# A single-core recurrent block: a written-out order of 2633 pieces of work, searched anew with other hand-over times

## The chip, the cores and the metric

The kernel runs on one NeuronCore of a Trainium2 chip. That core has a matrix engine (TensorE, PE in the profile, with its weight loads shown apart as PEld), a vector engine (DVE), an activation engine (ACT), a general-purpose engine (POOL) and a sync engine (SP) that here only issues transfers. Each engine works through its own instructions in the order in which they were emitted, and waits in front of an instruction until what it needs from other engines is there. The metric is the device time of one execution in microseconds; lower is better.

## The reference, cut to what matters

The block is one RWKV-like layer on 8 sequences of 256 tokens with 512 channels (32 heads of 16), all in fp32:

```python
xn = ln(x, ln1_w, ln1_b);  sx = token_shift(xn, state[:, 1])
xxx = tanh((xn + sx * maa_x) @ maa_w1).reshape(b, l, 5, 1, 32)
x5  = xn[:, :, None] + sx[:, :, None] * (maa_stack + (xxx @ maa_w2))
w = exp(-exp(time_decay + tanh(x5[:, :, 1] @ decay_w1) @ decay_w2))
r, k, v = x5[:, :, 3] @ Wr.T, x5[:, :, 0] @ Wk.T, x5[:, :, 2] @ Wv.T
g = silu(x5[:, :, 4] @ Wg.T)
def step(s, (r_t, k_t, v_t, w_t)):            # 256 steps, state 16 x 16 for each head
    a = k_t[..., :, None] * v_t[..., None, :]
    return a + w_t[..., None] * s, einsum("bhk,bhkd->bhd", r_t, u * a + s)
att = group_norm(outs) * gn_w + gn_b
x = x + (att * g) @ Wo.T
xn2 = ln(x, ln2_w, ln2_b);  sx2 = token_shift(xn2, state[:, 0])
rr = sigmoid((xn2 + sx2 * ffn_maa_r) @ Wfr.T)
kk = square(relu((xn2 + sx2 * ffn_maa_k) @ Wfk.T))
return x + rr * (kk @ Wfv.T)
```

## The kernel before, in words

**Three stages for each sequence.** The work of a sequence (a "batch" in the names, 0 to 7) is cut into three stages. `inputs_of_scan` makes the layer norm, the token shift, the five mixed inputs and the projections k, v, r, g and w. `scan` runs the recurrence in four blocks of 128 rows; each block has four groups, and for a group a broadcast load brings v from DRAM into a buffer `vs`, DVE multiplies it by k (L849), DVE scans over time (L851), POOL multiplies the scanned states by r (L854), and PE sums over the state with a selection matrix (the "gather", L862). `rest` makes the group norm, the product with Wo, the second layer norm and the feed-forward part. Stages of up to three sequences lie side by side in time.

**Pieces.** Nothing is issued where it is written. Each call (`plan.add`) notes a piece: an engine, an assumed duration, the buffers it writes and reads, and a function that issues it. There are 2633 pieces. Buffers come from small pools: six PSUM buffers `ps` for nearly all matmul results, one larger PSUM buffer `wrep` for the decay factors of the scan, six `vs` buffers, six `st8` buffers for scanned states (called `st` in the profile), fourteen `mix` buffers and some others. A piece that needs a buffer waits until its last user is done.

**What sets the order.** `order` is a list scheduler. It takes the ready piece with the lowest rank from a heap, gives it the earliest start that its engine, its inputs and its buffers allow, and picks the buffers. The ranks are a table of numbers, `TURNS`, one row for each stage. The earliest start is worked out with a few assumed times: `LATENCY` (from the end of a piece on one engine until another engine may start on its result), `AHEAD` (added where PE is the receiver), `GAP` (between two dependent pieces on one engine) and `SWITCH` (a change of the activation table on ACT, and of the tile shape on PE). In the end all pieces are sorted by the planned start and emitted so. Therefore the table and the assumed times set three things only: the order of the pieces on each engine, which buffer each piece gets, and, in `tiles`, whether a matmul with full-width weights is issued as one wide or four narrow instructions. On the chip an instruction starts when what it waits for is there, whatever the plan assumed.

**Names that follow.** The matmuls are issued by a helper, so most stand at one line (L398) and are told apart by tiles: `mix,mw` is the first mixing product of a batch (its result goes to `ta` by a tanh on ACT, L651), `ta,mw2a` the second, whose results ACT and DVE turn into the mixed inputs (L674, L676). `tb,mw2b` is the product for the fifth mixed input. `mix` with `Wk`, `Wv`, `Wr`, `Wg` are the projections, which ACT copies out of PSUM (L757, L787). `Ws` are streamed weights: with `g` it is the product with Wo, with `mix` the feed-forward products; ACT evacuates them with a relu (L943) or a sigmoid into `o` (L952). L912 to L928 belong to the group norm: ACT copies rows of the reciprocal (`sq`, `rk`, L917), POOL multiplies (L919, L928). ACT also makes `wrep` (L832), the first column of each `vs` (L842), and copies to `att` (L812). SP issues all loads and stores but `vo`, which ACT issues.

Of the kernel before, what the change touches and what calls it, by code (L numbers as in the profile page):

```python
# [67 lines left out]
class Plan:  # L68
# [4 lines left out]
    LATENCY = {"PE": 0.12, "DVE": 0.09, "ACT": 0.09, "POOL": 0.09, "DMA": 1.65}  # L73
    LANDS = {"vs__": (2.3, 1.8), "rsb_": (0.2, 1.9), "sq_": (0.2, 1.9), "s": (0.2, 1.9), "vo_": (0.75, 2.2), "vo__": (0.38, 2.2), "o_": (0.75, 1.1), "x": (1.6, 1.7), "xt": (1.6, 1.7)}
    SWITCH = {"ACT": 1.3, "PE": 0.12}
    AHEAD = {"PE": 0.2}
    GAP = {"PE": 0.0, "DVE": 0.16, "ACT": 0.04, "POOL": 0.11, "DMA": 0.03}
# [37 lines left out]
    def stage(self):  # L115
# [964 lines left out]
```

## Time and profile before

| | |
|---|---|
| median of 3 runs | 617.36 us (617.15 to 620.06) |
| profiled execution, its own time | 618.31 us |
| span of its trace | 616.4 us |
| granted TensorE clock | 1.00 |
| PE busy | 594.5 us, 96% |
| DVE busy | 542.2 us, 88% |
| POOL busy | 518.0 us, 84% |
| ACT busy | 511.6 us, 83% |
| PE busy between 50 and 550 us | 491.01 of 500 us |
| PE busy from 564 us on | 47.76 of 52.4 us |

Busy time is the sum of the time in which an engine executes; an engine waits in the rest. Where two numbers stand behind a row of the timeline they are the start and the length in microseconds; a bracket at the end of a row gives the idle time just before it and the engine and line that ended it. Rows of like instructions in a line are put together, with their number behind an x.

### The profile page before, as it was taken

Reading aid. Unit: us, or ns where it says so; the run is one execution under the profiler, and the core shown is the slowest. Engines: PE = TensorE matmul, PEld = TensorE weight load, DVE = VectorE, ACT = ScalarE, POOL = GpSimd, SP = SyncE. Lnnn points to the kernel's source line nnn. Section 1 sums busy time; section 2 is a strip of 40 time slices with the busy share of each in tenths; the row PEclk is TensorE's granted clock in tenths of the full one; section 3 lists DMA queues with packets and bytes.
Section 4 is the critical chain, followed back from the end, with each engine's and each line's share of the span. In section 5 each row is a group of like instructions: output and inputs, shape, how many; then the busy total and the mean of one; then the engine's idle time right before and its main releaser. Section 6 shows DMA issues by size and latency. Waiting matters only on the chain.

```text
span 616.4 us, 18782 instructions
## 1 busy us (share of the span) xinstructions
PE 594.5 (96%) x7856; PEld 341.6 (55%) x7856; DVE 542.2 (88%) x490; ACT 511.6 (83%) x1164; POOL 518.0 (84%) x414
## 2 busy tenths in 40 slices
PE   5999999899999999999999999999999999999997
PEld 5675556456544674367543664465754464446464
DVE  5689999999999998799989999999999999895441
ACT  3888679989999989989999888999889789965431
POOL 1799999999999988899889999999889998887030
PEclk9999999999999999999999999999999999999999
DMA  8897779687778787758787697677876698861542
GB/s 287 265 242 171 214 192 231 163 233 181 185 202 235 206 206 214 197 154 221 202 240 206 197 248 202 184 230 218 224 194 193 185 252 245 225 193 66 165 145 85
DMA packets 52499, 124.83 MB, mean 203 GB/s; under 512 B 5824, under 2 KB 11200, under 8 KB 52416
## 3 DMA queue, kind: packets, MB, share of 16 engines
q1 hardware_dynamic: 48048, 119.46, 71.4%
q10 hardware_dynamic: 4368, 4.20, 2.1%
q8 instruction: 61, 1.00, 0.7%
q14 instruction: 22, 0.18, 0.1%
HBM read 115.25 MB, written 8.39 MB: 201 GB/s over the span
## 4 chain that ended last, share of the span: by engine, by line
PE 61%; ACT 17%; DVE 7%; POOL 7%; DMA 5%; issue 3%; SPq 0%; ACTq 0%; DVEq 0%; POOLq 0%
PE ps L398 51%; PE ps L862 5%; DMA vs<-vo 4%; POOL st L854 4%; DVE st L851 3%; ACT sq L917 2%; ACT rk L917 2%; PE ps L574 2%; PE ps L726 2%; DVE vs L849 2%; ACT att L812 1%; ACT wrep L832 1%; ACT ps L674 1%; ACT mix L605 1%; ACT vs L842 1%
## 5 line engine op out<-in xcount | busy, mean ns | idle before, releaser
L851 DVE TENSOR_TENSOR_SCAN st<-wrep,vs 128x1024 f32<-128x1024 f32 x128 | 289.2, 2277 | 4.9 <-ACT wrep L832 1.9
L854 POOL TENSOR_TENSOR st<-st,r 128x1024 f32<-128x1024 f32 x128 | 254.3, 2003 | 11.0 <-DVE st L851 9.5
L849 DVE TENSOR_TENSOR vs<-vs,ps 128x1024 f32<-128x1024 f32 x122 | 143.7, 1205 | 9.7 <-ACT vs L842 8.5
L398 PE MATMUL ps<-Ws,mix 128*32 128x512 f32 (+2 forms) x864 | 114.9, 589 | 1.9 <-ACT o L952 1.0
L398 PEld LDWEIGHTS ps<-Ws,mix 128*32 128x32 f32 (+1 forms) x864 | 37.8, 116 | 65.3 <-issue 58.2
L686 POOL TENSOR_TENSOR mix<-mix,xn 128x512 f32<-128x512 f32 x62 | 66.6, 1095 | 2.8 <-DVE mix L680 2.0
L588 POOL TENSOR_TENSOR sx<-xn 128x512 f32<-128x512 f32 x30 | 31.5, 1061 | 38.0 <-ACT xn L584 37.9
L862 PE MATMUL ps<-st,con 128*32 128x256 f32 x1024 | 62.1, 381 | 1.2 <-POOL st L854 1.0
L398 PE MATMUL ps<-mix,Wv 128*32 128x256 f32 (+1 forms) x688 | 59.8, 380 | 0.0
L398 PE MATMUL ps<-mix,Wr 128*32 128x256 f32 (+1 forms) x760 | 59.3, 380 | 0.0
L398 PE MATMUL ps<-mix,Ws 128*32 128x256 f32 (+1 forms) x736 | 57.8, 380 | 1.3 <-issue 0.7
L398 PE MATMUL ps<-mix,Wk 128*32 128x256 f32 (+1 forms) x952 | 59.0, 379 | 0.0
L398 PE MATMUL ps<-mix,Wg 128*32 128x256 f32 (+1 forms) x712 | 58.7, 379 | 0.0
L398 PE MATMUL ps<-Ws,g 128*32 128x512 f32 (+1 forms) x464 | 56.7, 593 | 1.5 <-POOL g L928 1.5
L607 POOL TENSOR_TENSOR mix<-mix,xn 128x512 f32<-128x512 f32 x44 | 47.5, 1092 | 6.1 <-ACT mix L605 6.1
L398 PEld LDWEIGHTS ps<-mix,Ws 128*32 128x32 f32 (+1 forms) x736 | 42.0, 120 | 15.7 <-ACT o L952 1.5
L674 ACT ACTIVATE ps<-ps,vec 128x256 f32<-128x256 f32 x112 | 46.6, 444 | 4.6 <-PE ps L398 3.2
L398 PEld LDWEIGHTS ps<-mix,Wv 128*32 128x32 f32 (+1 forms) x688 | 40.6, 123 | 15.2 <-issue 1.0
L812 ACT COPY att<-ps 32x256 f32<-32x256 f32 x128 | 46.4, 363 | 2.8 <-POOL g L928 0.7
L862 PEld LDWEIGHTS ps<-st,con 128*32 128x32 f32 x1024 | 32.3, 110 | 29.5 <-issue 6.5
L398 PEld LDWEIGHTS ps<-mix,Wr 128*32 128x32 f32 (+1 forms) x760 | 38.7, 119 | 17.8 <-issue 0.8
L398 PEld LDWEIGHTS ps<-mix,Wg 128*32 128x32 f32 (+1 forms) x712 | 39.1, 122 | 16.7 <-ACT xn L584 0.6
(123 smaller groups left out, 952.5 us busy)
## 6 DMA issues: line engine op xcount, KB each, us to landing
vs<-vo SPq DMA_DIRECT2D x128, 512.0 KB, 5.8
Ws<-in_fr SPq DMA_DIRECT2D x16, 512.0 KB, 6.5
Ws<-in_wo SPq DMA_DIRECT2D x16, 512.0 KB, 5.6
Ws<-in_fk SPq DMA_DIRECT2D x16, 512.0 KB, 5.8
Ws<-in_fv SPq DMA_DIRECT2D x16, 512.0 KB, 5.4
x<-in_x SPq DMA_DIRECT2D x9, 512.0 KB, 6.3
vo<-v ACTq DMA_DIRECT2D x15, 256.0 KB, 4.9
out<-o SPq DMA_DIRECT2D x15, 256.0 KB, 4.7
```

What stands on the lines that cost most here:

```text
L398: nc.tensor.matmul(out[i : i + n], lhsT=w[:, i : i + n], rhs=x, start=first, stop=final)
L574: nc.tensor.transpose(ps()[:, m, n * P : (n + 1) * P], xh[n]()[:, k * P : (k + 1) * P], idt())
L588: take(512, [sx], [xn], lambda xn=xn, sx=sx, e=nc.vector if alone and q else nc.gpsimd: e.tensor_tensor(sx(), xn()[:, :, 0:T], xn()[:, :, ...
L607: gp(512, t, [t, xn[q]], lambda q=q, t=t: nc.gpsimd.tensor_tensor(t(), t(), xn[q]()[:, :, 1 : T + 1], ALU.add))
L674: act(256, p_, [p_, vec], lambda g=g, q=q, m=m, p_=p_: nc.scalar.activation(p_()[:, m, :], p_()[:, m, :], AF.Identity, bias=col(f"maa_{g}" ...
L686: gp(512, t, [t, xn[q]], lambda q=q, t=t: nc.gpsimd.tensor_tensor(t(), t(), xn[q]()[:, :, 1 : T + 1], ALU.add))
L812: act(350, atts[q], [pc], lambda i=32 * (2 * q + m), m=m, q=q, h=32 * h: nc.scalar.copy(atts[q]()[h : h + 32, m, :], pc()[i : i + 32, 0, :]))
L849: dve(4 * T, [vs], [vs, kp], lambda m=m, vs=vs, kp=kp: nc.vector.tensor_tensor(vs(), vs(), kp()[:, m : m + 1, :].to_broadcast([P, 4, T]), ...
L851: dve(4 * T, [st], [w, vs], lambda w=w, vs=vs, st=st: nc.vector.tensor_tensor_scan(st().rearrange("p n t -> p (n t)"), w().rearrange("p n ...
L854: gp(4 * T, st, [st, r], lambda m=m, st=st, r=r: nc.gpsimd.tensor_tensor(st(), st(), r()[:, m : m + 1, :].to_broadcast([P, 4, T]), ALU.mul ...
L862: nc.tensor.matmul(pat()[32 * i : 32 * i + 32, 0, :], lhsT=con()[:, s : s + 32], rhs=done[i]()[:, j, :], start=(j == 0), stop=(j == 3),)
L917: act(256, rsb, [rs], lambda blk=2 * q + n, n=n, rows=rows, rsb=rsb: nc.scalar.copy(by_block(rsb)[rows, n, :], rs()[32 * blk : 32 * blk + ...
```

## The change

Only assumed times and the ranks change. The pieces, their assumed durations, the pools and the code that issues them are the same; the table `TURNS` is replaced as a whole (its first two lines are shown).

```diff
-    LATENCY = {"PE": 0.12, "DVE": 0.09, "ACT": 0.09, "POOL": 0.09, "DMA": 1.65}
+    LATENCY = {"PE": 0.25, "DVE": 0.13, "ACT": 0.14, "POOL": 0.06, "DMA": 1.65}
-    SWITCH = {"ACT": 1.3, "PE": 0.12}
-    AHEAD = {"PE": 0.2}
-    GAP = {"PE": 0.0, "DVE": 0.16, "ACT": 0.04, "POOL": 0.11, "DMA": 0.03}
+    SWITCH = {"ACT": 1.38, "PE": 0.11}
+    AHEAD = {"PE": 0.1}
+    GAP = {"PE": 0.0, "DVE": 0.16, "ACT": 0.08, "POOL": 0.12, "DMA": 0.03}
...
     TURNS = """
-        7 135 8 30 33 47 70 145 79 48 121 116 189 225 137 147 149 159 4 5 16 6 34 35 36 37 43 31 38 56 32 46 60,
-        0 1 2 9 3 10 11 12 13 14 20 21 22 23 27 15 17 18 19 24 28 29 25 26 39 40 45 63 87 94 96 95 97 107 64 66 73 74
...
+        13 19 16 27 30 99 87 111 97 83 112 28 228 50 21 56 142 156 2 3 17 9 39 46 38 41 47 36 40 49 37 58 59,
+        0 1 4 5 6 7 8 10 11 12 23 31 32 34 35 14 18 22 24 25 42 43 29 33 44 45 48 65 103 104 108 105 107 116 66 78 80
...
```

What the two orders look like beside each other is shown at three places, which the prediction comes back to. In these rows the numbers behind a name tell buffers apart.

**Place 1: POOL ahead of the last gather of batch 0.** The names: `st` times `r` (L854) are the products behind the scan, `mix` plus `xn` (L686) are the mixed inputs of batch 2, `rk` (L799) and `att` (L818) belong to the scan of batch 1. Before:

```order
L686 TENSOR_TENSOR mix_109<-mix_109,xn_99 128x512
L818 TENSOR_TENSOR att_139<-v_129,att_139 128x2x256
L854 TENSOR_TENSOR st_156<-st_156,r_126 128x1024
L799 TENSOR_TENSOR rk_150<-r_125,k_124 128x512
L686 TENSOR_TENSOR mix_116<-mix_116,xn_99 128x512
L686 TENSOR_TENSOR mix_106<-mix_106,xn_99 128x512
L854 TENSOR_TENSOR st_157<-st_157,r_126 128x1024
L854 TENSOR_TENSOR st_152<-st_152,r_126 128x1024
L854 TENSOR_TENSOR st_153<-st_153,r_126 128x1024
```

and after:

```order
L686 TENSOR_TENSOR mix_109<-mix_109,xn_99 128x512
L686 TENSOR_TENSOR mix_113<-mix_113,xn_99 128x512
L854 TENSOR_TENSOR st_156<-st_156,r_126 128x1024
L686 TENSOR_TENSOR mix_116<-mix_116,xn_99 128x512
L854 TENSOR_TENSOR st_157<-st_157,r_126 128x1024
L854 TENSOR_TENSOR st_152<-st_152,r_126 128x1024
L854 TENSOR_TENSOR st_153<-st_153,r_126 128x1024
L686 TENSOR_TENSOR mix_117<-mix_117,xn_99 128x512
L799 TENSOR_TENSOR rk_150<-r_127,k_123 128x512
```

The product `rk` moved from ahead of the last three `st` products of that gather to behind them; one 128x512 piece less stands in front of them.

**Place 2: PE around the first mixing product of batch 4** (`mix,mw`). `Ws,mix` with 32x512 are the halves of the two sigmoid products of batch 1; `ta,mw2a` is the second mixing product of batch 4. Before:

```order
L398 MATMUL ps_174<-mix_111,Ws_165 32x256 x8
L398 MATMUL ps_174<-mix_118,Ws_166 32x256 x8
L398 MATMUL ps_169<-mix_107,mw_66 32x256 x8
L398 MATMUL ps_169<-mix_115,mw_66 32x256 x8
L398 MATMUL ps_170<-Ws_164,mix_110 32x512 x8
L398 MATMUL ps_170<-Ws_167,mix_106 32x512 x8
L398 MATMUL ps_174<-Ws_164,mix_110 32x512 x8
L398 MATMUL ps_174<-Ws_167,mix_106 32x512 x8
L398 MATMUL ps_173<-ta_120,mw2a 64x256 x2
L398 MATMUL ps_170<-ta_120,mw2a 64x256 x2
```

and after:

```order
L398 MATMUL ps_174<-Ws_164,mix_119 32x512 x8
L398 MATMUL ps_170<-Ws_164,mix_119 32x512 x8
L398 MATMUL ps_172<-mix_115,mw_66 32x256 x8
L398 MATMUL ps_172<-mix_113,mw_66 32x256 x8
L398 MATMUL ps_170<-Ws_165,mix_111 32x512 x8
L398 MATMUL ps_174<-Ws_165,mix_111 32x512 x8
L398 MATMUL ps_170<-ta_120,mw2a 64x256 x2
```

Two of the four halves moved ahead of the mixing product. In both orders the second mixing product writes to `ps_170` early, which the first sigmoid product had filled.

**Place 3: ACT around the two sigmoids of batch 2** (`o`), with the tanh of batch 5 (`ta`) near them. Before:

```order
L917 COPY sq_159<-sq_158 32x256 x6
L605 ACTIVATE mix_106<-sx_102,vec 128x256
L812 COPY att_138<-ps_169 32x256
L842 ACTIVATE vs_147<-s_82,cm_83 128x4
L787 ACTIVATE g_135<-ps_171 128x512
L952 ACT_TABLE_LOAD
L952 ACTIVATE o_162<-ps_173 128x512
L952 ACTIVATE o_163<-ps_170 128x512
L651 ACTIVATE ta_120<-ps_171 128x256
L832 ACT_TABLE_LOAD
L832 ACTIVATE wrep_168<-w_133 128x4x255
```

and after:

```order
L812 COPY att_138<-ps_169 32x256
L842 ACTIVATE vs_147<-s_81,cm_83 128x4
L812 COPY att_138<-ps_169 32x256
L917 COPY sq_159<-sq_158 32x256
L917 COPY rk_150<-sq_158 32x256
L952 ACT_TABLE_LOAD
L952 ACTIVATE o_162<-ps_172 128x512
L952 ACTIVATE o_163<-ps_170 128x512
L842 ACTIVATE vs_148<-s_81,cm_83 128x4
L832 ACT_TABLE_LOAD
L832 ACTIVATE wrep_168<-w_133 128x4x255
L812 COPY att_138<-ps_169 32x256
```

Three of the `att` copies that stood behind the sigmoids stand ahead of them now (a fourth was ahead already), and the tanh, which is the next row after those shown, comes behind `wrep`. The first mixing product of batch 5 (`ps_171` before) has `ps_170` now, the buffer that the second sigmoid frees.

234 rows, old and new, of the table TURNS are left out of this document.

## The prediction

> **What bounds the kernel now.** I read the busy line of the page first, then the busy time by stretches of the span, then PE's waits, and the timeline around each of them.
>
> ```profile
> PE 594.5 (96%) x7856; PEld 341.6 (55%) x7856; DVE 542.2 (88%) x490; ACT 511.6 (83%) x1164; POOL 518.0 (84%) x414
> ```
>
> ```profile
> 7.29:50.00 42.71, 41.76 (x512) 31.08 (x520) 33.14 (x55) 32.38 (x79) 30.74 (x29) 1.00 0.94 267
> 50.00:550.00 500.00, 491.01 (x7055) 273.12 (x7039) 477.50 (x392) 450.84 (x1035) 465.24 (x358) 1.00 0.78 208
> 550.00:564.00 14.00, 14.00 (x86) 11.69 (x79) 12.24 (x9) 8.56 (x19) 13.57 (x11) 1.00 0.19 57
> 564.00:616.40 52.40, 47.76 (x232) 25.70 (x224) 17.09 (x30) 18.25 (x31) 7.98 (x8) 1.00 0.40 135
> ```
>
> The columns are the stretch, its length, the busy time of PE, PEld, DVE, ACT and POOL, then clock, DMA share and GB/s. PE is the bound, and nearly nothing is left: it idles 500.00 − 491.01 = 9.0 us between 50 and 550, about 1 us of the 42.71 before, nothing in the 14 us before the last gather, and 4.6 us after 564, where the same pieces follow in almost the same order in both versions. DVE idles 22.5 us in the middle. A gain must therefore come out of PE's 9.0 us, and its waits show whom PE waits for:
>
> ```profile
> PE ps L398 <- ACT r L757: 1.9, 1, 1.9
> PE ps L398 <- issue: 1.6, 2, 0.9
> PE ps L398 <- POOL g L928: 1.5, 2, 0.9
> PE ps L398 <- ACT o L952: 1.2, 2, 1.0
> PE ps L862 <- POOL st L854: 1.0, 1, 1.0
> PE ps L574 <- ACT xh L558: 0.6, 1, 0.6
> PE ps L398 <- POOL mix L607: 0.5, 1, 0.5
> PE ps L398 <- ACT mix L943: 0.3, 1, 0.3
> ```
>
> (total, times, longest; 50 to 550 us). These are 8.6 of the 9.0 us, in eleven waits of 0.2 to 1.9 us. ACT and POOL are themselves nearly full there, 90% and 93%, so a wait ends when an in-order queue has worked off what stands ahead of one piece. That is what a new order changes.
>
> **What moves.** The work is the same. The tile form changes for a few full-width pieces (four narrow instructions or one wide for the same columns), and PE changes its tile shape 107 times instead of 105. A gather takes 1.73 us, and 1.86 behind a change:
>
> ```profile
> 56.23 1.73 PE ps L862 x32
> 501.33 1.86 PE ps L862 x32
> ```
>
> so the two changes cost 2 x 0.13, about **+0.2** (estimate). The number of table loads on ACT stays the same. Otherwise pieces change places by a few rows; the summed work ahead of each of the 32 gathers differs by under 4 us on PE and on DVE, mostly by nothing. So I go from wait to wait, count by durations of the trace what more or less stands ahead, and carry the waits on.
>
> *The gather at 96.75 (place 1).*
>
> ```profile
> 90.76 5.93 POOL L854 TENSOR_TENSOR st<-st,r 128x1024 f32<-128x1024 f32 x3
> 96.75 1.71 PE L862 MATMUL ps<-st,con 128*32 128x256 f32 x27 [1.04 <-POOL st L854]
> 88.38 4.46 DVE L851 TENSOR_TENSOR_SCAN st<-wrep,vs 128x1024 f32<-128x1024 f32 x2
> L686 POOL TENSOR_TENSOR mix<-mix,xn 128x512 f32<-128x512 f32 x62 | 66.6, 1095 | 2.8 <-DVE mix L680 2.0
> ```
>
> PE waits 1.04 us for the last of three products of POOL, which follow one another without a gap. One piece of 128x512 less (1.1 us by the group of L686, on average) stands ahead, so they end about 1.05 earlier; the last scan ends at 92.84 and leaves room for it (with one product of 5.93 / 3 = 2.0 us behind it, 94.8). **−1.0**; bounds −1.0 and 0, if POOL meets a late input there.
>
> *From 236 to 247 (place 2).*
>
> ```profile
> 236.09 1.93 PE L398 MATMUL ps<-mix,mw 128*32 128x256 f32 x32 [0.54 <-POOL mix L607]
> 237.84 7.05 PE L398 MATMUL ps<-Ws,mix 128*32 128x512 f32 x64
> 244.30 0.60 ACT L952 ACTIVATE o<-ps 128x512 f32<-128x512 f32 x1
> 245.01 1.12 PE L398 MATMUL ps<-ta,mw2a 32*64 32x256 f32 x32
> 247.16 1.06 PE L398 MATMUL ps<-Ws,mix 128*32 128x512 f32 x8 [1.03 <-ACT o L952]
> ```
>
> Two of the four sigmoid halves (7.05 / 4 = 1.76 each) move ahead of the mixing product, 3.5 us of work, while its input from POOL gets about 2.0 later (one more 2.0 us product ahead): the wait of 0.54 goes. But the next waits are set by ACT. Its first `o` gets about 0.5 later (`ta` moves back by about 0.85, one row copy of 0.40 goes from between). It ended at 244.90 and frees `ps_170`, so the second mixing product starts at about 245.5, though PE would be there at 244.5; the second `o`, on which 247.16 hangs, moves by the same 0.5. The 0.54 saved is waited off here, and 0.5 more: **+0.5**. Bounds: −0.5, if ACT is not late, and +0.9.
>
> *From 312 to 317 (place 3).*
>
> ```profile
> 309.92 1.28 ACT L952 ACT_TABLE_LOAD   x1
> 311.21 1.09 ACT L952 ACTIVATE o<-ps 128x512 f32<-128x512 f32 x2
> 312.35 3.66 PE L398 MATMUL ps<-mix,Ws 128*32 128x256 f32 x64 [0.17 <-ACT o L952]
> 312.65 1.28 ACT L832 ACT_TABLE_LOAD   x1
> 314.05 1.03 ACT L832 ACTIVATE wrep<-w 128x1020 f32<-128x1020 f32 x1
> 317.38 1.93 PE L398 MATMUL ps<-mix,Ws 128*32 128x256 f32 x32 [0.32 <-ACT mix L943]
> ```
>
> The pair of sigmoids gets three `att` copies (0.36 each by their record), two row copies and one small piece more ahead and three small pieces fewer, together about +1.1 us. The mixing product of batch 5 now goes into the buffer that the second sigmoid frees, at about 312.3 + 1.1 = 313.4, while PE comes there at about 312.2: a wait of 1.2 in place of 0.17. The tanh behind it goes back by 1.28 + 1.03 = 2.3 us and a copy, and its taker on PE comes behind products of 3.66 us, which cover that. I take **+0.5**, half, because I cannot see whether ACT, which has small waits of its own ahead, carries the whole 1.1 on; bounds −0.5 (both waits gone) and +1.6.
>
> *The other waits of PE.*
>
> ```profile
> 541.15 2.35 PE L398 MATMUL ps<-Ws,mix 128*32 128x512 f32 x20 [0.85 <-issue]
> 480.07 2.35 PE L398 MATMUL ps<-Ws,g 128*32 128x512 f32 x20 [0.93 <-POOL g L928]
> 136.17 1.09 PE L574 MATMUL ps<-idt,xh 128*128 128x128 f32 x8 [0.57 <-ACT xh L558]
> 115.42 0.69 PE L398 MATMUL ps<-tb,mw2b 32*64 32x256 f32 x16 [1.88 <-ACT r L757]
> ```
>
> The first row's releaser is not seen; the sigmoid that comes before it on ACT gets 3.4 us less ahead: **−0.85**, bounds −0.85 and 0. The other wait without a releaser (1.6 − 0.9 = 0.7, at 453) stands before a product whose two halves change places: **0**, bounds −0.7 and +0.7. At 480 the chain runs over ACT (affine, then POOL's product), with about 0.7 more ahead on ACT: **+0.3**, bounds 0 and +0.7. At 136 ACT has 0.3 to 0.5 more ahead: **+0.2**, bounds 0 and +0.5. At 115 PE makes r before k and v now, but on ACT both copies stand together behind the same `wrep`: **0**, bounds −1.9 (the wait goes) and +0.4.
>
> *Loads.*
>
> ```profile
> 92.86 9.60 DMA vs<-vo
> ACT vs L842 <- DMA vs<-vo: 2.0, 4, 0.9
> ```
>
> The load that the chain of waits shows with 9.60 us landed behind a load of x for the next product with Wo; in the new order that load of x goes out much earlier, into the head, and another one later. ACT waited 2.0 us in all, in four pieces of 0.5 on average; one of them moves: **−0.5**, bounds −2.0 and +0.6 (another load in the way, one more such piece). In the head the earlier order of the constants keeps its loads in time by my count, 0.
>
> **The sum**: +0.2 − 1.0 + 0.5 + 0.5 − 0.85 + 0 + 0.3 + 0.2 + 0 − 0.5 = −0.65 us. The profiled execution took 618.31 us, of which 616.4 are the span and 1.9 lie around it; it becomes 617.7. It lies 0.95 above the median of 617.36, and against that the sum gives **616.7 us**. About 0.5% (3.1 us) is what a measurement can tell from no change, so this is "the same". With all lower bounds the sum is −7.25, with all upper ones +5.6.
>
> **The rivals.**
>
> *R1, faster: the new times are truer, and the search finds what I cannot follow by hand.* For it speaks a hand-over in the head:
>
> ```profile
> 13.81 1.89 PE L398 MATMUL ps<-mix,mw 128*128 128x256 f32 x8
> 15.74 0.38 ACT L651 ACTIVATE ta<-ps 128x256 f32<-128x256 f32 x1 [0.29 <-PE ps L398]
> 16.17 0.67 PEld L398 LDWEIGHTS ps<-ta,mw2a 32*64 32x64 f32 x32 [0.22 <-ACT ta L651]
> L851 DVE TENSOR_TENSOR_SCAN st<-wrep,vs 128x1024 f32<-128x1024 f32 x128 | 289.2, 2277 | 4.9 <-ACT wrep L832 1.9
> ```
>
> The plan counts 1.728 us for the first piece, so ACT starts 15.74 − 13.81 − 1.728 = 0.20 behind its planned end: the old 0.12 is too short by 0.08, the new 0.25 too long by 0.05. From ACT to PE it is 16.17 − 15.74 − 0.315 = 0.115, of which the plans count 0.09 and 0.14 (and `AHEAD`). A scan (2277 ns on average, 2.200 planned) needs at least 0.08, with a hand-over more; the new 0.13 is nearer than 0.09. An order made with times that are too short puts PE's pieces just ahead of their inputs, as the eleven waits look. Without the wait of 1.9 at 115 and the second one on POOL's `g` (1.5 − 0.9 = 0.6), for which nothing ahead changes, 9.0 − 1.9 − 0.6 = 6.5 us could go, less 0.2 for the tile changes: 617.36 − 6.3 = **611.1 us**. Against it: what I could follow shows new waits of like size at ACT.
>
> *R2, slower: ACT's queue.* An evacuation that stands behind more pieces keeps its PSUM buffer longer, and PE stops at the next piece that takes it. The price is the upper bounds of place 3 (1.6), 115 (0.4), 136 (0.5), 236 to 247 (0.9), 480 (0.7) and the tile changes (0.2), with none of the gains: +4.3, **621.7 us**. It decides where ACT has no idle time of its own ahead of the piece; at place 3 it is so from 309.92 to 317.33. Against it: elsewhere ACT idles a tenth of the time and can catch up.
>
> *R3, DVE is the bound and the order of PE means nothing.* DVE is busy 477.5 of the middle 500 us, its work is the same in both orders, and a PE whose busy time hid slack would gain nothing by another order: the time stays at **617.4**. Against it: the pieces of PE follow one another at their own rate, 1.73 us for 32 instructions, through whole stretches, and DVE has 22.5 us idle in the middle to PE's 9.0. The Trainium skill ("Perfetto Trace Analysis", section "Identifying the Most-Contended Engine") warns that matmul busy time is no good measure of how near TensorE is to its limit and asks for MFU and the busy share of weight loads; by the page's 55% for PEld DVE would be the most contended engine at 88%, and the time would stay at 617.4. The 1.73 us per 32 instructions speak against it here.
>
> **How the numbers follow.** My sum 0.35, R1 0.33, R2 0.24, R3 0.08. R1 lies under 614.3, the bound of 0.5%; R2 above 620.4. Of the sum's own spread 0.02 ends on the faster and 0.01 on the slower side: faster 0.35, same 0.40, slower 0.25. The sum's own range is 614.5 to 619.5. The range of all holds R1's time with 2 us to spare and R2's with 0.6: 609.0 to 622.3.
>
> **What would show it.** PE's busy time in the middle tells all: 9.0 us idle now, 8 to 9 by my sum, about 2.5 by R1, 13 by R2. Step by step: the gather near 96 starts without a wait on POOL; the second mixing product of batch 4 and the sigmoid after it wait for ACT's `o`; the first mixing product of batch 5 waits about 1 us for `o`; the wait at 541 is gone. If PE's idle time falls and the span doesn't, R3 holds. I am wrong if waits of several us stand at a place that had none, above all at the start of the scan or for a load.

## The result, and the profile after

The changed kernel takes 624.52 us (median; 623.24 to 627.34), the kernel before 617.25 us measured beside it. The ratio is 1.0115, with a 95% interval of 1.0066 to 1.0163: the change makes the kernel slower by about 7 us. The profiled execution took 623.52 us with a span of 621.6, 5.2 more than before.

The busy line of the page and the stretches of the span of the changed kernel (columns as in the prediction: stretch, its length, busy time of PE, PEld, DVE, ACT and POOL, clock, DMA share, GB/s):

```profile
PE 596.1 (96%) x7736; PEld 348.6 (56%) x7736; DVE 543.3 (87%) x490; ACT 513.7 (83%) x1164; POOL 517.5 (83%) x414
```

```profile
7.29:50.00 42.71, 41.23 (x515) 30.27 (x519) 34.12 (x55) 32.81 (x80) 30.48 (x29) 1.00 0.91 266
50.00:75.00 25.00, 21.09 (x400) 11.92 (x388) 20.86 (x17) 18.75 (x43) 21.28 (x17) 1.00 0.62 150
75.00:300.00 225.00, 220.93 (x3100) 129.53 (x3096) 215.78 (x176) 206.59 (x481) 214.28 (x163) 1.00 0.78 206
300.00:550.00 250.00, 245.15 (x3372) 136.81 (x3364) 235.71 (x189) 222.12 (x499) 224.30 (x173) 1.00 0.77 209
```

The same stretches of the kernel before:

```profile
50.00:75.00 25.00, 24.82 (x479) 14.89 (x463) 25.00 (x22) 20.40 (x50) 25.00 (x18) 1.00 0.73 190
75.00:300.00 225.00, 219.16 (x3176) 126.92 (x3172) 212.14 (x173) 206.38 (x475) 212.57 (x164) 1.00 0.78 201
300.00:550.00 250.00, 247.03 (x3416) 131.31 (x3412) 240.36 (x199) 224.06 (x511) 227.67 (x177) 1.00 0.79 216
```

PE's idle time is the stretch less its busy time. The three stretches differ:

| stretch | before | after | difference |
|---|---|---|---|
| 50 to 75 us | 0.18 | 3.91 | +3.7 |
| 75 to 300 us | 5.84 | 4.07 | −1.8 |
| 300 to 550 us | 2.97 | 4.85 | +1.9 |

Between 50 and 75 us DVE and POOL, which had no idle time at all before, lose about 4 us too, and the DMA share falls. From 75 to 300 us the new order is the better one. From 300 us on it is the worse one. The sum of the three is 3.8 us. The busy time of PE grew by 1.6 us as well, for the same work. It grew in groups whose instructions are the same in number and shape, by 0.7 us each in the 800 narrow `Ws,mix` matmuls (90.1 to 90.8), the gathers (62.1 to 62.8) and `tb,mw2b` (5.5 to 6.2); what made them longer is not shown.

The waits of PE in the changed kernel, 50 to 550 us (total, times, longest):

```profile
PE ps L398 <- ACT g L787: 3.4, 1, 3.4
PE ps L398 <- ACT o L952: 2.1, 4, 1.0
PE ps L398 <- ACT k L757: 1.2, 2, 0.8
PE ps L398 <- DVE vs L849: 1.2, 1, 1.2
PE ps L726 <- ACT v L757: 1.1, 1, 1.1
PE ps L398 <- POOL g L928: 0.9, 2, 0.7
```

One wait of 3.4 us is new. It names ACT, which evaluated the silu of a product (`g`, L787) late and so freed PE's next buffer late. The timeline of the changed kernel around it, PE and ACT:

```profile
64.79 1.94 PE L398 MATMUL ps<-mix,mw 128*32 128x256 f32 x32 [3.45 <-ACT g L787]
57.69 0.30 ACT L842 ACTIVATE vs<-s,cm 128x4 f32<-128x4 f32 x1 [2.20 <-DMA vs<-vo]
62.96 0.30 ACT L842 ACTIVATE vs<-s,cm 128x4 f32<-128x4 f32 x1 [2.01 <-DMA vs<-vo]
64.14 0.60 ACT L787 ACTIVATE g<-ps 128x512 f32<-128x512 f32 x1
65.11 0.69 DVE L676 TENSOR_TENSOR mix<-ps,sx 128x512 f32<-128x512 f32 x1 [3.67 <-ACT ps L674]
```

ACT stood twice, 2.20 and 2.01 us, in front of a tiny piece that writes the first column of a `vs` buffer, because the load of that buffer had not landed; everything behind it on ACT stood too. Over the whole span these waits of ACT grew from the 2.0 us in four pieces that the prediction shows to 9.0 us in ten:

```profile
ACT vs L842 <- DMA vs<-vo: 9.0, 10, 2.2
```

So the question is why these loads were late. SP's own rows of the changed kernel, 36 to 51 us, and its wait for the store of v, 36 to 56 us:

```profile
36.17 0.52 SPq L387 DMA_DIRECT2D vs<-vo  x1
36.73 0.59 SPq L387 DMA_DIRECT2D Wg<-in_wg  x1
37.37 0.47 SPq L387 DMA_DIRECT2D x<-in_x  x1
50.31 1.85 SPq L387 DMA_DIRECT2D vs<-vo  x2
SPq L387 <- DMA vo<-v: 12.3, 1, 12.3
```

and of the kernel before, in the same stretches:

```profile
36.64 14.70 SPq L387 DMA_DIRECT2D vs<-vo  x4
SPq L387 <- DMA vo<-v: 9.4, 1, 9.4
```

In both kernels SP stops until about 50.2 us for the store of the second half of v, issued on ACT's queue at 41.6 (before) and 41.9 us (after), from which the loads of blocks 2 and 3 of batch 0 read. Before, all eight loads of blocks 0 and 1 are issued ahead of that stop, and DVE lives on them: the last two open the row at 36.64 (issued at 36.64 and 40.11), whose other two are issued behind the stop. After, only seven are. The new order on SP puts the first load of block 2 ahead of the last load of block 1, so this last load, which needs nothing from the store, is issued at 50.9 us, 10 us after its time. Ahead of the stop stands the load of x for the product with Wo in its place.

### The profile page after: what moved, and what is told of

Its sections match the earlier page's. It is cut to its first block, busy times and chain, and to the rows that moved or that the text cites. A ratio compares the mean times of both kernels' runs of the same rounds, so it can differ in the third digit from the quotient of the medians.

```text
span 621.6 us, 18554 instructions
## 1 busy us (share of the span) xinstructions
PE 596.1 (96%) x7736; PEld 348.6 (56%) x7736; DVE 543.3 (87%) x490; ACT 513.7 (83%) x1164; POOL 517.5 (83%) x414
## 4 chain that ended last, share of the span: by engine, by line
PE 46%; ACT 30%; DMA 8%; DVE 6%; issue 5%; POOL 5%; SPq 0%; ACTq 0%; DVEq 0%; POOLq 0%
PE ps L398 37%; DMA vs<-vo 6%; PE ps L862 5%; ACT rk L917 3%; ACT sq L917 3%; ACT ps L674 3%; ACT att L812 3%; ACT wrep L832 2%; DVE st L851 2%; ACT mix L605 2%; ACT vs L842 2%; PE ps L574 2%; POOL st L854 1%; ACT L832 1%; PE ps L726 1%
## 5 line engine op out<-in xcount | busy, mean ns | idle before, releaser
L854 POOL TENSOR_TENSOR st<-st,r 128x1024 f32<-128x1024 f32 x128 | 254.1, 2001 | 7.3 <-DVE st L851 6.7
L398 PEld LDWEIGHTS ps<-Ws,mix 128*32 128x32 f32 (+1 forms) x864 | 40.0, 116 | 62.5 <-issue 51.1
L686 POOL TENSOR_TENSOR mix<-mix,xn 128x512 f32<-128x512 f32 x62 | 67.0, 1099 | 4.7 <-DVE mix L680 3.9
L862 PE MATMUL ps<-st,con 128*32 128x256 f32 x1024 | 62.8, 381 | 1.0 <-ACT mix L943 0.4
L398 PEld LDWEIGHTS ps<-mix,Ws 128*32 128x32 f32 (+1 forms) x712 | 40.2, 122 | 16.5 <-issue 0.9
L398 PEld LDWEIGHTS ps<-mix,Wg 128*32 128x32 f32 (+1 forms) x640 | 41.2, 126 | 14.0 <-ACT r L757 0.4
```

The costliest lines, as they stand in the source:

```text
L398: nc.tensor.matmul(out[i : i + n], lhsT=w[:, i : i + n], rhs=x, start=first, stop=final)
L686: gp(512, t, [t, xn[q]], lambda q=q, t=t: nc.gpsimd.tensor_tensor(t(), t(), xn[q]()[:, :, 1 : T + 1], ALU.add))
L854: gp(4 * T, st, [st, r], lambda m=m, st=st, r=r: nc.gpsimd.tensor_tensor(st(), st(), r()[:, m : m + 1, :].to_broadcast([P, 4, T]), ALU.mul ...
L862: nc.tensor.matmul(pat()[32 * i : 32 * i + 32, 0, :], lhsT=con()[:, s : s + 32], rhs=done[i]()[:, j, :], start=(j == 0), stop=(j == 3),)
```

## The experiments

Each kernel changes the finished order by moving single pieces; hand-over times, ranks and pieces stay unless the edit says otherwise. The edit is one call behind the sort. `moved` takes each named piece out of the order and puts it ahead of or behind another; only its list of moves differs, and the diffs below show this list alone (cut out of the head of `moved`):

```diff
-        done.sort(key=lambda op: op.start)
+        done.sort(key=lambda op: op.start); self.moved(done)
```

Two theories stood at the start: L, the order of the loads in the head is the cause of the stall; Q, ACT's in-order queue is the cause, by the order of ACT's own pieces.

| kernel | median us | ratio to before, 95% interval |
|---|---|---|
| changed kernel | 624.52 | 1.0115 (1.0066 to 1.0163) |
| two loads swapped back | 620.50 | 1.0063 (1.0038 to 1.0088) |
| x loaded late | 622.27 | 1.0077 (1.0057 to 1.0096) |
| x and first half of Wo late | 624.44 | 1.0108 (1.0092 to 1.0124) |
| all three moves | 621.85 | 1.0065 (1.0043 to 1.0087) |
| swap and x late | 620.59 | 1.0038 (1.0017 to 1.0059) |
| one piece of ACT moved | 621.76 | 1.0063 (1.0045 to 1.0081) |
| before, with the loads swapped the wrong way | 622.97 | 1.0074 (1.0047 to 1.0100) |

The kernels ran in several rounds, each beside the kernel before, whose median lay between 617.25 and 618.17 us from round to round. So the ratios are the better comparison between rows.

**The two loads swapped back.**

```diff
+moves = (("DMA", "vs0_2_1", "behind", "vs0_1_1"),)
```

> The changed kernel with one load moved: the first load of block 2 of batch 0, which must wait for the store of v to land (50.2 us), goes behind the last load of block 1 instead of ahead of it. Theory L (SP's in-order queue and the load order in the head): the last load of block 1 no longer waits behind it, is issued at about 41 instead of 50.9 and lands at about 52 instead of 57.7; the gather of block 1 (74.7 us in the changed kernel, 70.8 before) comes 1 to 3 us earlier, total 622 to 623.5 instead of 624.5. Theory Q (ACT's in-order queue sets PE's stall of 3.4 us at 64.8, loads don't matter): 624.5 +- 0.7, and the gather stays at 74.7.

PE's stall of 3.45 us shrinks to 0.55 us (at 61.45), and the gather of block 1 starts at 71.37 us. The rows of the changed kernel and of this one:

```profile
74.71 1.94 PE L862 MATMUL ps<-st,con 128*32 128x256 f32 x32
```

```profile
71.37 1.93 PE L862 MATMUL ps<-st,con 128*32 128x256 f32 x32
50.00:75.00 25.00, 24.00 (x444) 13.79 (x448) 23.54 (x21) 20.23 (x47) 24.34 (x18) 1.00 0.68 157
75.00:300.00 225.00, 221.02 (x3108) 132.22 (x3101) 215.24 (x174) 206.69 (x478) 214.53 (x165) 1.00 0.78 207
300.00:550.00 250.00, 244.94 (x3340) 135.16 (x3336) 236.14 (x192) 222.63 (x502) 223.42 (x172) 1.00 0.78 208
```

One swap of two neighbouring loads gives 4.0 us back by the medians, more than theory L had allowed for, and 3.2 us by the ratios, whose intervals still overlap (1.0066 to 1.0088). The trace is the stronger evidence: PE idles 1.0 us now from 50 to 75 us instead of 3.91; the other two stretches hardly change (3.98 and 5.06 us).

**x loaded late, and the first half of Wo too.** The diffs are these moves; "all three moves" has both and the swap.

```diff
+moves = (("DMA", "x20", "ahead", "vs1_1_1"),)
+moves = (("DMA", "x20", "ahead", "vs1_1_1"), ("DMA", "Wo0_1", "ahead", "Wo0_0"))
```

> The changed kernel with one load moved: x for the product with Wo of batch 0 is loaded late (beside the loads of block 1 of batch 1), not in the head. Theory L: one transfer of about 2.2 us less lies ahead of the store of v, which lands at about 48 instead of 50.2; all that hangs on it comes 2 us earlier, the gather of block 1 at about 72.7, total about 622.5. Theory Q: 624.5 +- 0.7.

> As the run before, and the first half of Wo is loaded beside its second half, not in the head. Theory L: two transfers of 2.2 us less in the head, the loads of the scan land up to 4.4 us earlier and the store of v at about 46 to 47; gather of block 1 at about 71, total 620 to 621. Theory Q: 624.5 +- 0.7.

> All three moves together. Theory L: the gather of block 1 at 70.8 us or earlier, as before the change, total 619.5 to 621, so that 4 of the 7 us lost come back and the rest has another cause. Theory Q: 624.5 +- 0.7.

The first came as theory L said: one transfer less ahead of the store, which landed at 48.0 us, and 2.2 us gained. The second missed by 4 us. In its profile the first of the two stores of the first half of v landed at 24.7 instead of 26.2 us; SP then issued three loads of `vs` instead of one before the second of these stores went out, the store stood behind their transfers, and the loads that read from it waited for it on SP. The median time to landing of these two small stores, in a view of the transfers of each queue from 20 to 36 us, of the changed kernel and of this one:

```profile
vo<-v ACTq DMA_DIRECT2D x2, 128.0 KB, 4.0
```

```profile
vo<-v ACTq DMA_DIRECT2D x2, 128.0 KB, 5.2
```

The second of the two stores landed at 31.6 us in the changed kernel and at 35.5 in this one. Taking traffic out of the head was no gain by itself; it also counted what stood in front of a store on which SP's queue waits. That the move of Wo brought this about is not shown: the same three loads ahead of the second small store, and a landing at 34.8 us, stand in the profile of the swap with x late below, where Wo's load stays in the head. All three moves together missed as well: 621.85 us, no better than the swap alone, with the gather of block 1 at 74.10 us instead of 70.8.

**Swap and x late.**

> The changed kernel with the two loads swapped back and x for the product with Wo of batch 0 loaded late, the first half of Wo staying in the head. Theory L: the store of v lands at about 48, the last load of block 1 at about 50, and the loads of block 2 2 us earlier than with the swap alone; total 618.5 to 620. If the swap alone had already taken the loads off the path: 620.5 +- 0.5.

By its median it equals the swap alone, and the intervals of the two ratios overlap: once the two loads stand in the old order, no cost of the early load of x can be told from nothing. Its interval (1.0017 to 1.0059) lies wholly below that of the change. But the way to that time was not theory L's. The profiled execution took 624.38 us, one of two of the ten above 624. In it the store of v, issued at 42.3 us, took 9.5 us to land, not until 51.8 us instead of 48, and the stall is back although the two loads stand in the old order. Its rows on ACT and PE:

```profile
62.85 0.30 ACT L842 ACTIVATE vs<-s,cm 128x4 f32<-128x4 f32 x1 [3.79 <-DMA vs<-vo]
64.69 3.43 PE L398 MATMUL ps<-mix,mw 128*32 128x256 f32 x32 [2.93 <-ACT g L787]
```

The load that ACT waits for here went out behind the store, at 53.2 us, and took 9.7 us. So the swap takes one late load away; where the store lands later and the next load takes long, PE stalls all the same. In the kernel before with one piece of POOL moved (below) SP goes on as late, at 51.8 us, and no such stall stands there: other moves of the new order have a part in it, which no run separated.

**One piece of ACT moved**, with the loads as in the changed kernel:

```diff
+moves = (("ACT", "vs0_2_2", "behind", "g0_0"),)
```

> The changed kernel with one small piece of ACT moved: the first column of the third load of block 2 of batch 0, at which ACT stood until the load landed (62.9 us), goes behind the silu that frees PE's next buffer. PE's stall of 3.45 us at 64.8 should shrink by about 2 us in both theories. Theory L (the late loads set the pace, the stall is only where it shows): the gather of block 1 and the total stay, 624 +- 0.7. Theory Q (ACT's in-order queue is the cause): total 622 to 622.5.

The rows of this kernel where the stall and the gather of block 1 were:

```profile
61.94 0.64 PE L398 MATMUL ps<-mix,mw 128*32 128x256 f32 x8 [0.50 <-ACT g L787]
72.88 1.93 PE L862 MATMUL ps<-st,con 128*32 128x256 f32 x32
```

Here theory L as I had put it was wrong. The loads are nearly as late as in the changed kernel (SP's stop for the store ends at 49.6 instead of 50.3 us), and yet 2.8 us come back by the medians: PE's wait falls from 3.45 to 0.5 us, and the gather of block 1 comes 1.8 us earlier. The late load costs time because ACT stands in order in front of it, with a copy behind it for which PE waits. Loads and ACT's queue are one chain, not two theories.

**The kernel before, with the loads swapped the wrong way.** A first try of this moved the load of block 2 forward past a scan that still read its buffer; in that kernel this scan multiplies data of the wrong block, and its 627.81 us say nothing. The second one moves the other load back:

```diff
+moves = (("DMA", "vs0_1_0", "behind", "vs0_2_2"),)      # on the kernel before
```

> The kernel before with one load moved: the last load of block 1 of batch 0 goes behind the first load of block 2, which waits for the store of v to land. Nothing else changes, all results stay. Theory L: that last load goes out at 50.8 instead of 40.1 us and lands at about 57 instead of 49.7; the gather of block 1 (70.8 us) comes 2 to 4 us later, ACT stands at the first column of that buffer, PE stalls behind ACT, total 619.5 to 621.5. Rival (the loss belongs to the new order of the other engines, not to this pair of loads): 617.4 +- 0.7.

One moved load on the kernel before costs 5.0 us by the medians (4.6 by the ratio), 1.5 us above the upper end of theory L's range. PE's waits of this kernel from 50 to 75 us, and its stretch:

```profile
PE ps L862 <- POOL mix L686: 3.5, 1, 3.5
50.00:75.00 25.00, 21.45 (x368) 12.41 (x360) 21.05 (x16) 18.12 (x43) 22.53 (x16) 0.93 0.68 159
```

The place at which PE stands is another (a gather), the stall is of the same size. Part of the 5.0 us is not the stall itself: the granted clock in this stretch is 0.93, and the gather behind the stall took 3.55 us in place of 1.93. The order of this pair of loads brings a stall of about 3.5 us in either order of the rest. Taking it back took the stall away in the profile of the swap alone, though not in that of the swap with x late.

**Ranks and hand-over times apart.**

> The kernel before with the new hand-over times and its own old ranks; the order on SP stays as before, pieces on the other engines shift by a row here and there and get other buffers. Theory T (the loss sits in the searched ranks, the constants alone matter little): 617 to 619. Theory C (the constants spoil the plan): 621 or more.

> The changed kernel's ranks with the old hand-over times; the order on SP is that of the changed kernel. Theory T: the loss stays, 623 to 626, with the gather of block 1 of batch 0 near 74.7. Theory C: 617 to 620.

The old ranks with the new times: 618.67 us, ratio 1.0007 (0.9995 to 1.0020). The new times alone change nothing. The new ranks with the old times: 628.91 us, 1.0182 (1.0148 to 1.0216), slower than the change itself. The loss sits in the new ranks, as theory T said; that they do worse still with the old times it had not foreseen, and the old ranks do as well with either set.

**What the waits of PE are worth.** The swap leaves 2.8 us unexplained by the head, and the forecast had added up waits. The first test takes one wait away near 313 us (place 3), on top of the swap:

```diff
+moves = (("DMA", "vs0_2_1", "behind", "vs0_1_1"), ("ACT", "o2_0", "ahead", "o2_1"),
+         ("ACT", 2167, "behind", "o2_1"), ("ACT", 2159, "behind", "o2_1"), ("ACT", 1378, "behind", "o2_1"),
+         ("ACT", 1377, "behind", "o2_1"), ("ACT", 1491, "behind", "o2_1"))
```

> The changed kernel with the two loads swapped back (620.5 us) and ACT's pieces near 310 us put in another order: the second sigmoid of batch 2, whose product is done first and whose buffer the next mixing product takes, goes ahead of the first, and both go ahead of one small piece, two copies for att and two copies of reciprocals. Theory P (each wait of PE counts in full): PE's wait of 0.96 us at 313.3 goes and the total falls by 0.7 to 1.0, to 619.5 to 619.8. Rival (DVE or ACT sets the pace there and takes it back): 620.5 +- 0.4.

621.95 us, ratio 1.0068 (1.0043 to 1.0093): no gain. The wait of 0.96 us at 313.3 is gone, and two others stand behind it, rows of this kernel's timeline:

```profile
316.95 1.12 PE L398 MATMUL ps<-ta,mw2a 32*64 32x256 f32 x32 [0.78 <-ACT ta L651]
318.42 3.66 PE L398 MATMUL ps<-mix,Ws 128*32 128x256 f32 x64 [0.34 <-ACT mix L943]
```

0.78 + 0.34 = 1.12 us: ACT had the same work to do before the tanh and the relu, in whatever order. Then the same question on the kernel before, with place 1 of the change, with a piece of ACT at 115 us, and with both:

```diff
+moves = (("POOL", "rk1_0", "behind", "st80_3_1"),)
+moves = (("ACT", "r2_0", "ahead", "wrep1_1"),)
+moves = (("POOL", "rk1_0", "behind", "st80_3_1"), ("ACT", "r2_0", "ahead", "wrep1_1"))
```

> The kernel before with one piece of POOL moved: the product rk of batch 1 goes behind the last product of the gather at 96.75 us, as in place 1 of the change. Nothing else changes. Theory P (a wait of PE that goes is a gain in full): the wait of 1.04 us on POOL at 96.75 goes and the total falls by 0.8 to 1.1. Rival M (the time is handed to the next waits, which ACT's and DVE's queues set): the wait goes, waits behind it grow, total within 0.4 of before.

> The kernel before with one piece of ACT moved: the copy of r of batch 2 out of PSUM goes ahead of the wide exponential that stood in front of it (1.02 us). PE's wait of 1.88 us at 115.42 should shrink to about 0.9. Theory P: total -0.7 to -1.0. Rival M: the wide exponential is late for DVE's scan, or the next waits grow; total within 0.4 of before.

> Both moves of the two runs before. Theory P: -1.6 to -2.0 us against before, about 615.7. Rival M: within 0.5 of before.

618.25, 618.07 and 617.77 us against 617.95, with ratios of 1.0006 (0.9988 to 1.0025), 1.0002 (0.9990 to 1.0013) and 1.0000 (0.9984 to 1.0016). None is a gain that can be measured, and the gains that theory P named lie outside all three intervals (which reach down to −0.7, −0.6 and −1.0 us). In the first, the wait at 96.75 went and another took its place 2.5 us later; in the last, the wait at 96.75 went, that at 115 shrank from 1.88 to 0.83 us, and the one at 478 grew from 0.93 (at 480). Rows of the two kernels:

```profile
99.21 1.94 PE L398 MATMUL ps<-mix,Wv 128*32 128x256 f32 x32 [1.27 <-ACT g L787]
```

```profile
478.45 7.07 PE L398 MATMUL ps<-Ws,g 128*32 128x512 f32 x64 [1.53 <-POOL g L928]
```

The profiled execution of the last had a span of 614.8 us, 1.6 less than that of before, which is what adding waits would give; its twelve timed executions lie between 616.52 and 621.20 and don't bear it out. Nor does its timeline: at the gather of block 1 (70.04 against 70.84 us), ahead of both moves, it already led by 0.8 us. At the product behind the wait at 453 it led by 2.2, so that the waits did count that far; 0.6 of this went at 478. Where the kernel stands at 70 us, at the end of the loads of the head, differs by as much between two profiles as one wait is worth, and a single profile of this kernel can't tell 1.5 us.

**New ranks first, old ranks last.** Since the new order was ahead from 75 to 300 us, two kernels take the new ranks for the early stages (with the loads swapped back) and the old ones for the rest, with the new times:

> New hand-over times, the two loads swapped back, the new ranks for the head and for every stage that begins before stage group 4 (about the first 240 us), the old ranks for the rest. Theory P (waits of PE add up): the first part has the new order's shorter waits (0.1 us ahead of before at 222 us), the rest those of before: 617.0 to 617.8. If the late loss of the new order came from the new hand-over times and not from the ranks, it would be 619 or more.

> As the run before, with the new ranks for one stage group more (about the first 300 us). The new order with the loads swapped back was 0.7 us ahead of the kernel before at 295 us. Theory P: 616.3 to 617.0, a little faster than before. If the late loss came from the new hand-over times: 619 or more.

Both missed: 633.18 us, ratio 1.0240 (1.0215 to 1.0266), and 623.44 us, 1.0085 (1.0068 to 1.0101). New waits stand where the two tables meet, between 227 and 270 us in the first kernel and between 300 and 360 us in the second. The first row is from the waits of PE in the first kernel, 50 to 300 us, the second from the timeline of the second kernel:

```profile
PE ps L398 <- DVE mix L676: 5.8, 2, 3.0
```

```profile
305.40 7.07 PE L398 MATMUL ps<-Ws,mix 128*32 128x512 f32 x64 [1.73 <-POOL mix L607]
```

Behind that both go at about the pace of before. The three waits of before at 453, 480 and 541 us stand in both, 12.8 us later each time in the first kernel and 4.4 to 4.7 us later in the second. No version beat the kernel before.

## Why the prediction was wrong, point by point

**The step that failed is the term for the loads**, −0.5, with its sentence that in the head the loads stay in time (0). ACT's waits for these loads were to fall from 2.0 us to 1.5; they rose to 9.0, and 4.2 of them stand between 50 and 75 us, where there had been none. The term measured +3.7 us of idle PE in that stretch, 3.2 to 4.0 us by the swap and 4.6 to 5.0 by the reverse swap. Its upper bound was +0.6, and all upper bounds together, +5.6, come to 623.0 us, less than the 624.52 measured. The prediction's own sign of being wrong, a wait of several us for a load at the start of the scan, is what came. I had followed the loads of constants and of x as transfers that need to land before their users. I did not ask, for each load on SP's queue, what the load in front of it waits for. The row of SP's waits for the store of v (9.4 us before) was there to be read. The landing of this store is also what the plan gets wrong: it takes 8.4 us from its issue at 41.64 in the kernel before and 8.3 from 41.89 in the changed one, with a DMA share of 0.86 and 0.78 meanwhile, where the median of its kind before is 4.9. With x loaded late it took 5.8, with the swap as well 9.5. The assumed landing times were not among the numbers that the change corrected.

**R2 had the right chain and the wrong place.** Its price was 621.7 us, from ACT standing behind more of its own pieces at five places. ACT's in-order queue did carry the loss to PE, but what ACT stood behind was a load, at a place that was not in the list.

**Place 1** was right: the wait of 1.04 us on POOL is gone. That this is worth 1.0 us was wrong, or can't be shown: the same move alone on the kernel before gave +0.3 us, within its interval.

**Place 2** was right in mechanism: the wait on POOL's `mix` is gone, and the second mixing product waits for `o`. Size and sign were off. The forecast was +0.5. The waits after, in the kernel with the loads swapped back, are 0.58 at the second mixing product, 0.43 behind the sigmoid and 0.29 behind a relu ahead of both, 1.3 us together, against 0.54 + 1.03 = 1.57 before: −0.3.

**Place 3** was right in mechanism, and its size came out by luck: the first mixing product of batch 5 waits for the second sigmoid, by the row of the changed kernel

```profile
316.93 1.94 PE L398 MATMUL ps<-mix,mw 128*32 128x256 f32 x32 [0.96 <-ACT o L952]
```

where I had worked out 1.2 and taken half, for the case that ACT does not carry the whole delay on. It carried nearly all of it. The net came to 0.96 − 0.17 − 0.32 = +0.47 us because the wait on the relu at 317.38 went, which the forecast had kept.

**The other waits.** At 115 us 1.17 + 0.78 = 1.95 us stand in place of 1.88: no change, as forecast. At 541 the wait is gone, as forecast. At 480 it is 0.68 instead of 0.93, and at 136 the wait is gone; I had both longer. A new one of 1.08 us stands in front of the decay product (ACT's `v`) and one of 0.67 at 306.7 (ACT's `g`), which no term held. From 300 us on the idle time rose by 1.9 us; my terms there came to −0.05.

**The method, adding waits, is the deeper fault.** In the four kernels that took a wait away, others grew behind it: on the same queue in one (ACT's `o`, then ACT's `ta` and `mix`), on another in the rest (POOL's `st` at 96.75, then ACT's `g` at 99.21; ACT's `r` at 115, then POOL's `g` at 479). My lower bound of −7.25 and R1's 611.1 us rested on that addition; no kernel came below the kernel before by more than its interval allows. That the fullness of ACT and POOL, nine tenths, is the reason is argued, not shown.

**R3** (DVE the bound) was not tested by a run of its own. The time did not stay at 617.4, but from 50 to 75 us DVE lost as much as PE, 4.1 us, so this stretch tells nothing between them. Nor do the kernels in which a wait of PE went without a gain: R3 would have them so as well.

**The rest of the 7 us** is not settled. The swap leaves 2.8 us by the medians and 3.9 by the ratio. In the profiles, whose spans differ by 2.1, PE is busy 1.4 us longer over the whole span; it idles 1.0 longer from 50 to 550 us (10.0 against 9.0) and a little less outside. Which of the other moves does it was not separated.

## What to carry to other kernels

On an in-order queue that issues loads, read for each load what the one in front of it waits for: a load that is ready goes out no earlier than the slowest wait ahead of it ends. Here one swap of neighbours was worth 3 to 5 us. The sum over the waits of a bound engine was no forecast here, where the engines that feed it are nearly full themselves: a wait that is removed can come back at a later piece, on the same queue or another. When times of a plan are corrected, check the landing of stores too; the plan's numbers for it stayed as they were, and no run tried whether a truer one helps.

## What the runs showed of the hardware that was not expected

In some profiles TensorE's granted clock falls to half after PE has had little to do: to 0.50 from about 118.3 to 121.7 us in the kernel with x loaded late, 3.4 us. It does not come in every execution. In the kernel with the new ranks and the old times, PE stood for 3.11 us, and the stretch after the stall shows a mean clock of 0.62; 32 matmuls took 2.98 us in place of 1.94:

```profile
64.00:68.00 4.00, 3.77 (x44) 2.05 (x48) 3.45 (x3) 3.58 (x11) 2.26 (x2) 0.62 0.11 24
64.23 2.98 PE L398 MATMUL ps<-mix,mw 128*32 128x256 f32 x32 [3.11 <-ACT g L787]
```

Stalls of 2.93 (swap and x late), 3.20 (x and first half of Wo late) and 3.53 us (the reverse swap) were followed by such a stretch too. The changed kernel's stall of 3.45 us was not in its profiled execution; of its four timed executions, the two without a drop (mean clock 1.00) took 623.24 and 623.52 us, the two with 0.995 and 0.993 took 625.52 and 627.34. By the two without a drop the change costs about 6 us. The swapped kernel doesn't show such a price: 620.38 and 623.97 us at 1.00 against 620.42, 620.50 and 621.34 at 0.997. The Trainium skill ("TensorE: Matmul & The Clock Gate", section "Part 1: The HAM clock gate (the "warmup" mystery)") says that the clock is at half after an idle window of about 3.4 us, and that the window runs freely. A stall of 3.45 us without a drop agrees with a free window, which it need not fill. The drops after 2.93, 3.11 and 3.20 us do not agree with a wholly idle window of that length. And in the kernel with x loaded late a drop follows two waits of 1.17 and 0.78 us with four matmuls between them:

```profile
115.79 0.65 PE L398 MATMUL ps<-tb,mw2b 32*64 32x256 f32 x4 [1.17 <-DVE vs L849]
117.22 0.68 PE L398 MATMUL ps<-tb,mw2b 32*64 32x256 f32 x12 [0.78 <-ACT k L757]
117.83 3.20 PE L398 MATMUL ps<-mix,Wv 128*32 128x256 f32 x32
118.00:122.00 4.00, 4.00 (x48) 2.03 (x44) 2.83 (x3) 3.93 (x10) 4.00 (x4) 0.57 0.56 142
```

PE was never idle for more than 1.17 us here. The product after it took 3.20 us in place of 1.93. The landing of one and the same store of 256 KB was the other surprise: it took from 5.8 us (x loaded late) to 9.7 (the kernel before with one piece of POOL moved), with a median of its kind of 4.9 us in the kernel before.
